# Moving a pair of heads between partitions in sixteen DMAs, with the values three score units behind

## The chip, the cores and the metric

One core of a Trainium2 chip. The metric is the device time of one execution in microseconds (us); less is better. The core has five engines that run at the same time, each through its own list of instructions in order, and wait for one another through semaphores: PE (TensorE, matrix products; PEld is its weight load), DVE (VectorE), ACT (ScalarE), POOL (GpSimd) and SP (SyncE, which here only issues DMAs). Sixteen DMA engines carry the data between the device's memory and the on-chip memory (SBUF), and between places of SBUF. SBUF and PSUM, where PE's results land, have 128 partitions.

## What is computed

One decoder layer for an input x of 8 x 512 x 512 and a context of 8 x 512 x 1024, all float32: a self-attention over the first axis with relative positions, a cross-attention with 8 heads of 64, and a hidden layer of 2048, each followed by an addition and a normalization. The parts that the change touches:

```python
src_trans = einsum('bsf,of->bso', src, W_src) + b_src       # src: the context
tgt_trans = einsum('btf,of->bto', tgt, W_tgt) + b_tgt       # tgt: x after the self-attention
...
scores = einsum('bthd,bshd->bhts', q, k) / sqrt(64)
scores = where(src_mask[:, None, None, :] == 0, -inf, scores)
attn = softmax(scores, axis=-1)
tgt_update = einsum('bhts,bshd->bthd', attn, v).reshape(b, t, 512)
out = einsum('btf,of->bto', concatenate([tgt, tgt_update], axis=2), W_out) + b_out
...
h = relu(einsum('bsd,hd->bsh', x, w1) + b1)                 # then rounded to 8 bits, times w2
```

## The kernel before

There are two phases. The first (to line 617) does the self-attention and projects the context of the sequences 0 to 6 into keys and values; they are kept in the device's memory (`kd`, `vd`), as is the normalized result of the self-attention (`x1d`). The second phase (from line 630) is a loop over the eight sequences t, called steps here. The change is in the second phase.

The second phase is a pipeline over the steps, with an order written out by hand: the scheduler keeps the order in which the program emits instructions on PE, DVE, ACT and SP. In step t, PE does the attention of sequence t, the output projection of t-1 (`project_out`, lines 865 and 869), the query projection of t+1 (`queries`, line 729), the hidden layer of t-1 (`hidden_steps`, line 942) and the second product of the hidden layer of t-2 (`finish`, line 1020). `weave` (line 1091) mixes two lists: `dense` (projections and hidden layer) and the attention steps, which are spread over the dense work by weights; a number with each attention step says how much of the dense list must have been emitted before it.

**Attention.** A sequence has four pairs of heads, c = 0 to 3. A pair is worked on in two units, jj = 0 and 1, each for half of the 512 queries, with the number u = 2 (4t + c) + jj. `scores` (line 740) emits the four products of a unit (line 751) at once and puts the rest on a list of side work: `exponentials` (mask and row minimum on DVE, line 763, exponential on ACT, line 773), `divide` (line 788) and `turn_blocks` (line 800: DVE transposes 32 x 32 blocks within their 32 partitions into `pb`). `run` (line 673) pops side work ahead of each step by a credit of 0.7 of the step's cost, and `settle` (line 659) pops it until a given unit is done.

The blocks of `pb` must then change partitions: `move_blocks` (line 805) issues sixteen DMAs on SP's queue for each unit, one from each quarter g of the 32 partitions to each quarter a, into its half (jj) of `pT`. A pool has two `pb` (one for each unit) and one `pT`. The moves of a unit go on the list `moves`, and `move()` (line 669), which runs ahead of each step, emits them when the pair before has been emitted as attended (`moves[0][0] // 2 <= attended`). `attend` (line 836) makes the sixteen products of the pair (line 845, called av) from pT and the pair's values, and ACT copies the result to `uT`. In `attention_of` (line 1121) the attend of pair c follows the first unit of the pair after it; the last pair of a sequence is attended in the next step.

**Loads on SP's queue.** `load_kv` (line 714) loads a pair's keys and values into two buffers each; `attend_next` (line 1115) emits it for the pair after next, right behind the attend that frees the values' buffer. `load_x1` (line 710) loads `x1d` into one of three buffers; the buffer is free when the results of the sequence three before it have been stored from it (line 1045). The stores of line 1045 are side work of `finish`, and `settle(("y", t - 2))` emits them. `load_w1` (line 917) loads one of eight tiles of the first hidden weight (n = 0 to 7, 896 KB, prepared for a fast product with seven submatrices) into a ring of three (`ring`, part of the tile `ffn`); it is emitted in `p13`, the first products of tile n-2. In step 0 the tiles are loaded raw, POOL makes the sums (line 136 ff) and they are stored in `w1d` (lines 926 to 931); later they come from `w1d` (line 922). SP's list is in order: a DMA that waits for its buffer holds all that are behind it.

**Step 0** has no output projection or hidden layer. Its dense work is the context projection of sequence 7 in eight pieces (`project_context`), between them four conversions of the second hidden weight to 8 bits (`convert`, each of which issues the next load), and the queries of sequence 1. The weights `w_src` for these pieces and the ring `ffn` use the same memory (pool `big`, one buffer), so the ring is taken, and its first two tiles are loaded, at the end of step 0 (lines 1237 to 1257).

Of the kernel before, what the change touches and what calls it, by code (L numbers as in the profile page):

```python
# [42 lines left out]
def decoder_layer(  # L43
# [586 lines left out]
    with ExitStack() as ph:  # L630
# [11 lines left out]
        pbp = pool("pb", 2)  # L642
# [23 lines left out]
        moves = []  # L666
        attended = 0

        def move():
            while moves and moves[0][0] // 2 <= attended:  # L670
                moves.pop(0)[1]()

# [22 lines left out]
        x1, x1T, qT, uT, mb, mvb, kT, v, pT, x2T, hq, mvc = ({} for _ in range(12))  # L695
# [18 lines left out]
        def load_kv(t, c):  # L714
            kT[t, c] = kvd.tile([P, S], F32, tag="kT", name=f"kT{t}_{c}")
            nc.sync.dma_start(kT[t, c], kd[t][:, c, :])
            v[t, c] = kvd.tile([P, ST, P], F32, tag="v", name=f"vx{t}_{c}")
            nc.sync.dma_start(v[t, c], vd[t][:, :, c * P : (c + 1) * P])
# [21 lines left out]
        def scores(t, c, jj):  # L740
            if c == 0 and jj == 0:
                uT[t] = qx.tile([P, EC, S], F32, tag="uT", name=f"uT{t}")
# [4 lines left out]
            for j in js:  # L747
# [10 lines left out]
                pss.append(ps)  # L758

# [32 lines left out]
            def turn_blocks(i):  # L792


                if i == 0:
                    prs.append(
                        pbp.tile([P, 4, ST, 2, 2, 32], F32, tag="pb", name=f"pb{u}")
                    )
                for h in range(2):
                    nc.vector.transpose(  # L800
                        prs[4][:, :, :, h, i, :].rearrange("p a k e -> p k a e"),
# [3 lines left out]
            def move_blocks():  # L805

                if jj == 0:
                    pT[t, c] = ptp.tile(
                        [P, 4, 2, ST, 2, 64], F32, tag="pT", name=f"pT{t}_{c}"
                    )  # L810
                for a in range(4):
                    for g in range(4):
                        nc.sync.dma_start(  # L813
                            pT[t, c][32 * a : 32 * a + 32, g, jj],
                            prs[4][32 * g : 32 * g + 32, a].rearrange(
                                "p k h j e -> p k h (j e)"
# [14 lines left out]
            side.append((u, 1.2, lambda: turn_blocks(0)))  # L831
            side.append((u, 1.2, lambda: divide(1)))
            side.append((u, 1.2, lambda: turn_blocks(1)))
            side.append((u, 0.0, lambda: moves.append((u, move_blocks))))

        def attend(t, c):
# [4 lines left out]
            attended += 1  # L841
            av = mm(f"av{t}_{c}")
# [90 lines left out]
        def hidden_steps(t):  # L933
# [38 lines left out]
            def p13(n):  # L972
                if t * HH2 + n + 2 < T * HH2:
                    load_w1(t * HH2 + n + 2)
# [6 lines left out]
            def p6(n):  # L981
                product(x[n], n, S2, tx[:, 1], False)
# [392 lines left out]
```

## Time and profile before

| | us |
|---|---|
| median of 3 runs (lowest, highest) | 2418.19 (2417.45, 2428.72) |
| the profiled execution | 2425.11 |
| its span | 2423.3 |
| first scores of step 0 (PE, line 751) | 941.7 |
| first second product of the hidden layer in steps 2, 3, 4, 5, 6, 7 (PE, line 1020) | 1279.9, 1451.4, 1618.8 ... 1953.2, 2120.3 |

A table of the stretches of the second phase, from the view that gives the busy time of each engine by stretch (us; PEclk is the clock that PE was granted, as a share of full speed):

| stretch | length | PE busy | DVE busy | ACT busy | PEclk | DMA share |
|---|---|---|---|---|---|---|
| 925 to 1117 (step 0) | 192 | 137.1 | 76.4 | 39.1 | 0.85 | 0.52 |
| 1117 to 1300 (step 1) | 183 | 148.3 | 88.4 | 55.7 | 0.91 | 0.43 |
| 1467 to 1635 (a middle step) | 168 | 148.0 | 90.1 | 57.7 | 0.95 | 0.43 |
| 2135 to 2310 (step 7) | 175 | 133.6 | 79.3 | 48.6 | 0.88 | 0.39 |
| 2310 to 2423 (the end) | 113 | 103.5 | 41.4 | 26.8 | 0.98 | 0.17 |

How to read it: PE is the busiest engine in every stretch. In the middle steps, which repeat, about 20 of 168 us are gaps between its products, and part of its busy time is at a lower clock. The profile says for each gap which event ended it, and the chain that ended last says which work or wait, in order of time, made up the span. A line of the timeline has its start, its duration, the engine, the line of the program, the operation with its output and inputs, how many there were in a row, and in brackets the idle time before it and what ended that.

### The profile page before, as it was taken

What the parts mean: (1) busy time and instruction counts of PE and PEld (TensorE: products, weight loads), DVE (VectorE), ACT (ScalarE), POOL (GpSimd) and SP (SyncE); (2) the same over time, 40 slices, a digit from 0 to 9 for tenths busy, and PEclk for the clock granted to TensorE, in tenths of its full rate; (3) what the DMA queues carried; (4) which work ended last, traced back from release to release, by engine and by line L of the source; (5) the groups of instructions that cost most, each with busy time, mean ns of one, the idle gap of its engine ahead of it and who ended that gap; (6) DMA issues with size and microseconds to landing.
All of it is one profiled execution on the core that took longest, in us unless ns stands there. A gap on an engine that the chain in (4) does not pass through costs nothing.

```text
span 2423.3 us, 22413 instructions
## 1 busy us (share of the span) xinstructions
PE 2130.3 (88%) x7552; PEld 1220.6 (50%) x7552; DVE 1518.1 (63%) x2542; ACT 592.2 (24%) x1325; POOL 167.9 (7%) x156
## 2 busy tenths in 40 slices
PE   8999999999999998866868899898898898996798
PEld 5654664664576665322443463453554544633456
DVE  4799999989999943453436355554564464554324
ACT  2011112001111112221322241332333332413312
POOL 1001100110010000021110001000000000000000
PEclk9999999999999999987989899999999998998899
DMA  8131530342242475533345253453443542633412
GB/s 295 38 109 35 198 141 22 126 145 72 87 161 73 149 254 178 153 97 102 102 142 142 76 167 93 120 143 94 130 129 84 165 133 68 177 75 109 129 35 94
DMA packets 165827, 293.38 MB, mean 121 GB/s; under 512 B 26832, under 2 KB 55504, under 8 KB 165712
## 3 DMA queue, kind: packets, MB, share of 16 engines
q1 hardware_dynamic: 149488, 263.33, 36.1%
q10 hardware_dynamic: 16224, 28.61, 3.2%
q8 instruction: 60, 0.98, 0.2%
q14 instruction: 55, 0.45, 0.1%
HBM read 165.49 MB, written 59.24 MB: 93 GB/s over the span
## 4 chain that ended last, share of the span: by engine, by line
PE 55%; DVE 19%; SPq 11%; DMA 10%; issue 3%; ACT 2%; POOL 0%; DVEq 0%; ACTq 0%; POOLq 0%
SPq L813 10%; PE hx L942 7%; PE av L845 6%; PE px L539 6%; PE pox L865 3%; DVE pv L428 3%; PE hz L942 3%; PE pox L869 3%; PE pz L539 3%; PE o L1020 3%; PE s L751 3%; PE ps_q L338 3%; PE psq L729 3%; PE po L454 2%; DMA pT<-pb 2%
## 5 line engine op out<-in xcount | busy, mean ns | idle before, releaser
L845 PE MATMUL av<-pT,vx 128*64 128x512 f32 x512 | 153.1, 753 | 148.5 <-DMA pT<-pb 148.5
L773 ACT ACTIVATE pe<-pe,nmax 128x512 f32<-128x512 f32 x256 | 183.3, 716 | 237.3 <-DVE nmax L763 227.9
L763 DVE CUSTOM_DVE_ANT_0 pe<-s,mb 128x512 f32<-128x512 f32 x256 | 167.8, 683 | 75.7 <-PE s L751 75.7
L845 PEld LDWEIGHTS av<-pT,vx 128*64 128x64 f32 x512 | 45.9, 172 | 244.4 <-issue 212.5
L800 DVE STREAM_TRANSPOSE pb<-pe 128x512 f32<-128x512 f32 x256 | 166.1, 687 | 1.5 <-issue 1.5
L942 PE MATMUL hx<-ffn 128*128 128x256 f32 x512 | 139.4, 395 | 24.9 <-DVE tm L996 21.7
L428 DVE TENSOR_TENSOR pv<-v,sc 128x2048 f32<-128x2048 f32 x64 | 148.5, 2320 | 2.0
L379 DVE TENSOR_TENSOR pq<-qw,k 128x2048 f32<-128x2048 f32 x64 | 147.3, 2302 | 1.1
L388 DVE TENSOR_REDUCE sc<-pq 128x64 f32<-128x2048 f32 x64 | 146.1, 2282 | 1.4
L942 PE MATMUL hx<-x2T,ffn 128*128 128x256 f32 x512 | 138.3, 393 | 3.7 <-ACT ffn L983 3.7
L751 PE MATMUL s<-kT,qTx 64*128 64x512 f32 x512 | 130.4, 625 | 8.3 <-DVE nmax L763 8.3
L942 PEld LDWEIGHTS hx<-ffn 128*128 128x128 f32 x512 | 91.1, 191 | 73.0 <-DVE tm L996 38.6
L865 PE MATMUL pox<-w_xo,x1Ts 128*128 128x512 f32 x256 | 123.3, 626 | 0.0
L454 PE MATMUL po<-w_o,aoT 128*128 128x512 f32 x256 | 121.7, 620 | 0.7 <-ACT aoT L451 0.7
L979 DVE TENSOR_TENSOR ffn<-hx,ffn 128x256 f32<-128x256 f32 x64 | 27.2, 424 | 150.8 <-PE hx L942 128.7
L788 DVE TENSOR_SCALAR pe<-pe,rden 128x512 f32<-128x512 f32 x256 | 116.3, 497 | 4.5
L729 PE MATMUL psq<-x1Ts,w_tgt 128*128 128x512 f32 x256 | 114.5, 597 | 4.7 <-ACT x1Ts L724 4.7
L338 PE MATMUL ps_q<-w_in,xt 128*128 128x512 f32 x256 | 116.8, 594 | 0.5 <-DVE qw L365 0.5
L869 PE MATMUL pox<-w_xo,uT 128*128 128x512 f32 x256 | 115.1, 592 | 0.0
L338 PE MATMUL ps_k<-w_in,xt 128*128 128x512 f32 x256 | 113.9, 593 | 0.0
L942 PEld LDWEIGHTS hx<-x2T,ffn 128*128 128x128 f32 x512 | 90.5, 190 | 46.5 <-issue 14.0
L338 PE MATMUL ps_v<-w_in,xt 128*128 128x512 f32 x256 | 111.6, 594 | 0.0
(180 smaller groups left out, 3231.7 us busy)
## 6 DMA issues: line engine op xcount, KB each, us to landing
pT<-pb SPq DMA_DIRECT2D x1024, 64.0 KB, 2.0
ffn<-w1d SPq DMA_DIRECT2D x56, 896.0 KB, 4.7
ch<-in_ctxT_dram SPq DMA_DIRECT2D x56, 256.0 KB, 3.3
td<-tx SPq DMA_DIRECT2D x28, 384.0 KB, 3.3
tx<-td SPq DMA_DIRECT2D x28, 384.0 KB, 5.2
r<-in_x_dram SPq DMA_DIRECT2D x32, 256.0 KB, 3.5
xt<-in_xT_dram SPq DMA_DIRECT2D x32, 256.0 KB, 2.6
x1d<-r ACTq DMA_DIRECT2D x32, 256.0 KB, 3.8
```

The source lines that it names most:

```text
L338: nc.tensor.matmul(ps, lhsT=xt[:, e, :], rhs=w_in[:, e, part * E : (part + 1) * E], start=(e == 0), stop=(e == EC - 1),)
L428: nc.vector.tensor_tensor(pr, v_all[:, :, fs].rearrange("p s (h d) -> p s h d", d=D1), sc[:, t, g * HH * T : (g + 1) * HH * T] .rearrange( ...
L454: nc.tensor.matmul(po, lhsT=aoT[:, c * P : (c + 1) * P], rhs=w_o[:, c, :], start=(c == 0), stop=(c == EC - 1),)
L539: nc.tensor.matmul(bank[:, first], lhsT=w7[:, a, f, ps] if part == 0 else b[f][:, ps], rhs=b[f] if part == 0 else w7[:, a, f, :], start=st ...
L729: nc.tensor.matmul(ps, lhsT=w_tgt[:, e, o * P : (o + 1) * P], rhs=x1T[t][:, e, :], start=(e == 0), stop=(e == EC - 1),)
L751: nc.tensor.matmul(ps[:, h, :], lhsT=qT[t][half[h], c, j * P : (j + 1) * P], rhs=kT[t, c][half[h], :], start=True, stop=True,)
L773: nc.scalar.activation(pe, pe, AF.Exp, bias=nmax[:, h : h + 1], scale=-1.0, accum_out=den[:, h : h + 1],)
L813: nc.sync.dma_start(pT[t, c][32 * a : 32 * a + 32, g, jj], prs[4][32 * g : 32 * g + 32, a].rearrange("p k h j e -> p k h (j e)"),)
L845: nc.tensor.matmul(av[half[h], :], lhsT=v[t, c][:, s, half[h]], rhs=pT[t, c][:, :, :, s, h].rearrange("p g i q -> p (g i) q"), start=(s == 0),
L865: nc.tensor.matmul(po, lhsT=x1T[t][:, e, js], rhs=w_xo[:, e, :], start=(e == 0), stop=False)
L869: nc.tensor.matmul(po, lhsT=uT[t][:, e, js], rhs=w_xo[:, EC + e, :], start=False, stop=(e == EC - 1),)
L942: nc.tensor.matmul(ps[:, 0:W], lhsT=ring[:, (t * HH2 + n) % RING, a, e, :], rhs=b[:, e, :], start=start and e == 0, stop=e == 1, skip_grou ...
```

## The change

- `pb` holds a whole pair (both units) and has one buffer in place of two; the sixteen moves are issued once for a pair. Each moves 32 partitions x 4 KB where each moved 32 x 2 KB, and the order of the quarters is rotated (g = (a + i) % 4).
- A pair's attend follows the second unit of the pair after it, so its values are three units behind its scores; the weights in `attention_of` are set anew, and the second unit of a step may be emitted ahead of the last attend of the step before. `divide` and `turn_blocks` change places.
- Keys and values are loaded apart, each put on a list `later` and issued two calls of `move()` later: the keys after the pair's second score unit, the values after its attend. `load_w1` goes from `p13` to `p6`, the step behind it.
- `x1` of the sequence t+1 is loaded inside step t from step 1 on (before: from step 2 on), and one transpose of it (`turns[1]`) goes behind the last output projection.
- Two of the eight context pieces of sequence 7 go from step 0 to step 1, and the ring is taken (`take_ring`), with its first two tiles, behind them.
- The buffer of `uT` is taken in `attend` and not in `scores`; a list `pb` of the bias is renamed `pbo`.

```diff
-        pbp = pool("pb", 2)
+        pbp = pool("pb", 1)
...
-        moves = []
+        moves, later = [], []
         attended = 0
 
         def move():
-            while moves and moves[0][0] // 2 <= attended:
+            while moves and moves[0][0] <= attended:
                 moves.pop(0)[1]()
+            for item in later:
+                item[0] -= 1
+            while later and later[0][0] < 0:
+                later.pop(0)[1]()
...
+            p = u // 2 + 2
+            if jj == 1 and p < T * EC:
+                later.append([2, lambda: load_k(p // EC, p % EC)])
...
             def turn_blocks(i):
-                if i == 0:
-                    prs.append(
-                        pbp.tile([P, 4, ST, 2, 2, 32], F32, tag="pb", name=f"pb{u}")
+                if i == 0 and jj == 0:
+                    pb[t, c] = pbp.tile(
+                        [P, 4, 2, ST, 2, 2, 32], F32, tag="pb", name=f"pb{t}_{c}"
                     )
...
             def move_blocks():
-                if jj == 0:
-                    pT[t, c] = ptp.tile(
-                        [P, 4, 2, ST, 2, 64], F32, tag="pT", name=f"pT{t}_{c}"
-                    )
-                for a in range(4):
-                    for g in range(4):
+                pT[t, c] = ptp.tile(
+                    [P, 4, 2, ST, 2, 64], F32, tag="pT", name=f"pT{t}_{c}"
+                )
+                for i in range(4):
+                    for a in range(4):
+                        g = (a + i) % 4
                         nc.sync.dma_start(
-                            pT[t, c][32 * a : 32 * a + 32, g, jj],
-                            prs[4][32 * g : 32 * g + 32, a].rearrange(
-                                "p k h j e -> p k h (j e)"
+                            pT[t, c][32 * a : 32 * a + 32, g],
+                            pb[t, c][32 * g : 32 * g + 32, a].rearrange(
+                                "p i k h j e -> p i k h (j e)"
                             ),
                         )
...
             side.append((("e", u), 1.0, lambda: exponentials(1, 1)))
-            side.append((u, 1.2, lambda: turn_blocks(0)))
             side.append((u, 1.2, lambda: divide(1)))
-            side.append((u, 1.2, lambda: turn_blocks(1)))
-            side.append((u, 0.0, lambda: moves.append((u, move_blocks))))
+            side.append((u, 1.3, lambda: turn_blocks(0)))
+            side.append((u, 1.3, lambda: turn_blocks(1)))
+            if jj == 1:
+                side.append((u, 0.0, lambda: moves.append((u // 2, move_blocks))))
...
             def p13(n):
-                if t * HH2 + n + 2 < T * HH2:
-                    load_w1(t * HH2 + n + 2)
...
             def p6(n):
+                if t * HH2 + n + 2 < T * HH2:
+                    load_w1(t * HH2 + n + 2)
...
             if p < T * EC:
-                load_kv(p // EC, p % EC)
+                later.append([2, lambda: load_v(p // EC, p % EC)])
...
-                    need = queried if u == 2 * EC else begun + (t > 0)
-                    weight = 0.5 if u % 2 == 0 else 1.0
-                    if u == 2 * EC - 1 and t in (0, T - 1):
-                        weight = 3.0
-                    steps += [(2.0, need, lambda n=n: scores(*n), weight)]
-                if u % 2 == 0 and u < 2 * EC:
-                    c = u // 2 - 1
-                    steps += [(3.8, projected, lambda c=c: attend_next(t, c), 0.5)]
+                    need = queried if u == 2 * EC else begun + (u > 1 and t > 0)
+                    steps += [[2.0, need, lambda n=n: scores(*n), 1.0]]
+                if u % 2 == 1 and u > 1:
+                    steps[-1][3] -= 0.7
+                    f = lambda c=u // 2 - 1: attend_next(t, c)
+                    weight = 2.2 if u == 2 * EC - 1 and t + 1 == T else 0.7
+                    steps += [(3.8, projected, f, weight)]
...
-                    early = 0 if t == 1 else NJ if t + 1 < T else NJ // 2
-                    if early:
-                        dense += sum(done[: early - 1], [])
+                    early = NJ if t + 1 < T else NJ // 2
+                    first = sum(done[: early - 1], [])
+                    second = done[early - 1]
+                    if t == 1:
+                        first = of(6.9, pieces[-2])
+                        second = of(6.9, pieces[-1]) + of(0.0, take_ring)
+                    dense += first
                     begun = len(dense)
-                    dense += values_of(t - 1)
-                    if early:
-                        dense += done[early - 1]
-                    dense += out4[0]
+                    dense += values_of(t - 1) + second + out4[0]
                     dense += of(0.0, settle, ("y", t - 2)) + out4[1]
-                    if 1 < t < T - 1:
+                    if t + 1 < T:
                         dense += of(0.0, load_x1, t + 1)
-                    dense += out4[2] + turns[0] + turns[1] + out4[3]
+                    dense += out4[2] + turns[0] + out4[3] + turns[1]
```

## The prediction

> **What bounds the kernel now.** I read the busy times and the chain that ended last, then who waits for whom on PE, then PE and SP side by side over one pass of the loop over t (a step).
>
> ```profile
> PE 2130.3 (88%) x7552; PEld 1220.6 (50%) x7552; DVE 1518.1 (63%) x2542; ACT 592.2 (24%) x1325; POOL 167.9 (7%) x156
> PE 55%; DVE 19%; SPq 11%; DMA 10%; issue 3%; ACT 2%; POOL 0%; DVEq 0%; ACTq 0%; POOLq 0%
> ```
> PE is the bound, yet SP's queue and DMA make up 21% of the chain. The PE waits say where:
>
> ```profile
> PE av L845 <- DMA pT<-pb: 148.5, 21, 30.7
> PE xtr L723 <- DMA x<-x1d: 28.6, 5, 6.1
> PE hx L942 <- DVE tm L996: 21.7, 42, 0.5
> ```
> Total, times, longest. 177 us are waits for two transfers: the turned probabilities pT, and the next x1. The third row (0.5 us each) is inside the hidden layer and not touched. PE's timeline in step 4:
>
> ```profile
> 1499.24 1.97 PE L723 MATMUL xtr<-ident,x 128*128 128x128 f32 x8 [5.68 <-DMA x<-x1d]
> 1501.00 5.11 PE L865 MATMUL pox<-w_xo,x1Ts 128*128 128x512 f32 x8
> 1549.76 6.36 PE L845 MATMUL av<-pT,vx 128*64 128x512 f32 x16 [7.18 <-DMA pT<-pb]
> 1587.80 3.65 PE L845 MATMUL av<-pT,vx 128*64 128x512 f32 x16 [2.00 <-DMA pT<-pb]
> ```
> The gap is in brackets. After 7.18 us of idling the same av takes 6.36 instead of 3.65 us; after 5.68 us, pox takes 5.11 instead of its usual 3.60 and xtr 1.97 instead of 1.3. After 2.00 us nothing is lost. So a wait over some 3 us costs another 2.2 to 2.7 us. SP's timeline of the same step:
>
> ```profile
> 1483.10 10.27 SPq L813 DMA_DIRECT2D pT<-pb  x16
> 1493.41 0.58 SPq L712 DMA_DIRECT2D x<-x1d  x1
> 1557.70 10.49 SPq L813 DMA_DIRECT2D pT<-pb  x16
> 1568.29 4.42 SPq L922 DMA_DIRECT2D ffn<-w1d  x2
> ```
> Sixteen moves (one of a pair's two units) hold the queue for 10.3 us: 0.64 us each. x1 is issued behind such a burst, at 1493.41, and PE, ready for it at 1493.56, waits until it lands.
>
> **The moves: 512 of 128 KB for 1024 of 64 KB.** At 0.64 us each, a pair costs SP 10.3 us instead of 20.6, 32 x 10.3 = 330 us of queue less, none of it PE time by itself. That holds if twice the bytes do not slow them:
>
> ```profile
> pT<-pb SPq DMA_DIRECT2D x1024, 64.0 KB, 2.0
> ffn<-w1d SPq DMA_DIRECT2D x56, 896.0 KB, 4.7
> x<-x1d SPq DMA_DIRECT2D x8, 1024.0 KB, 5.9
> ```
> ```profile
> 1516.00:1523.00 7.00, 7.00 (x19) 2.96 (x19) 2.92 (x6) 0.75 (x2) 0.29 (x1) 1.00 0.46 106
> ```
> The last two figures are DMA share and GB/s inside a burst: 0.46 and 106. From 64 KB in 2.0 us to 1024 KB in 5.9 is 4.1 us per MB, so 64 KB more are 0.3 us; and 128 KB per 0.64 us are 205 GB/s, what a stretch with ffn in it moved (201 at a share of 0.72). No row shows 4 KB pieces. Lower bound of a pair's burst: 9.4 us (16 issues at their 0.59 us median). Upper: 20 us, if 106 GB/s were all that these copies reach. I take 10.3 us plus 2.3 to land, since a share of 0.46 leaves room for twice the bytes.
>
> **Three units behind.** By the compiled order both score units of the next pair now stand ahead of each av, before only the first. A burst starts when the pair's last transpose is done and av of the pair before has ended, whichever is later, and lands 12.6 us on. Counting PE's own durations (o 3.45, s 1.92, av 3.59, pox 6.87, psq 3.45, a hidden product 0.87 us) from the step's first o, call it 0: av of pair 0 comes at 52 with its burst over at 38; av of pair 1 at about 90, its burst over at 73; pairs 2 and 3 have 14 us or more in hand. So in steps 2 to 6 the av waits go: 9.2 us plus 2.7 of slow clock.
>
> **What is behind the bursts now.** x1: the last transpose of pair 0 ends at 25.5 (scores at 12.3, three evictions, o's 2.4 us on DVE, division, 4 x 0.65); burst to 36; vx 0.6; four stores to 38.4. The x1 buffer is the one these stores read, so its load waits for their landing, 2.4 us: issue at 40.5, landing 46.3 (5.8 later, as in the rows above). PE wants it at 43.8: 2.5 us of idling, no clock loss, for 5.7 + 2.2 before. Bounds 0 to 6.
> The w1 load: it is issued a step later (p6), which puts the load for n=4 behind pair 2's burst. That burst begins 5.2 us after av of pair 1 (one product, ACT's copy and DVE's c12, transposes, tm, transposes stand in DVE's order): 15.5 us after av the load is issued, at 20.2 it lands (4.7). PE comes to hy of n=4 after 15 products, one s and two 0.5 us waits: 16.1. A new wait of 4.2 us, with 2.2 of slow clock 6.4. Before, the same load at 1568.29 was in time for hy at 1575.73, and PE had lost its time at av instead. Bounds 0 (the burst begins with av's end) to 12.
> A middle step is 167.4 us (1467.22 to 1634.62); less 9.2 + 5.7 + 2.7 + 2.2 it is 147.6; plus 2.5 + 6.4 it is 156.5. Four such steps gain 10.9 each, step 2 (171.6 us) gains 15.1: **58.7 us**.
>
> **pb with one buffer.** DVE's transposes of the next pair wait for the whole burst to land, and everything behind them on DVE waits too. In the steps above they come 3 to 5 us after landing, or hold only adds that PE doesn't need for 2 us. Cost 0; without that margin it is the excess, at the c11 add of the hidden layer.
>
> **Steps 0 and 1.** The longest wait is the end of step 0:
>
> ```profile
> 1109.47 6.34 PE L845 MATMUL av<-pT,vx 128*64 128x512 f32 x16 [30.72 <-DMA pT<-pb]
> ```
> ```profile
> 1092.61 0.91 SPq L712 DMA_DIRECT2D x<-x1d  x1
> 1093.62 14.20 SPq L813 DMA_DIRECT2D pT<-pb  x16
> ```
> SP spent 1075.11 to 1092.13 on two w1 tiles (loads, POOL's sums, stores), and the pair's last burst stood behind. They move behind the last context piece in step 1. From s at 941.66 to step 2's first o at 1279.85 are 338.2 us; waits for pT (46.2 + 23.8), w1 (5.8) and some 18 of slow clock are 94, leaving 244. New: step 0 becomes a chain per pair (burst 12.6, then four transposes, four exponentials, divisions, four transposes, some 12 us on DVE: 25 us for some 24 us of PE work), and the last conversions of w2 wait for a load behind a burst: I take 20 us of waits in all (10 to 40). Step 1: the two w1 tiles hold SP 17 us after the last context piece, so burst and x1 come later; x1 lands some 10 us after PE wants it, with clock 12. n=4's load goes through POOL here (8.4 instead of 4.7 us): 8 + 2. 244 + 20 + 12 + 10 = 286: **52 us**, and I take **48** for what is counted roughly here.
>
> **Step 7.** From 2120.3 to 2310.3 it takes 190.0 us; four waits for pT (4.0, 12.7, 13.3, 3.55) and 11 of slow clock go. Here n=4's load stands ahead of the burst and n=5's lands 3 us early; the last av (at 130 us) comes as its burst lands. 190 - 33.6 - 11 = 145.4, with 2 for that close call 147: **43 us**. The end (113 us) has no pT.
>
> **Sum.** 58.7 + 48 + 43 = 150 us. The profiled execution took 2425.1 us (span 2423.3): 2275. It lies 6.9 us over the median 2418.2, so 2268 is forecast.
>
> **Rivals.**
> (a) The new waits do not come: av of pair 1 finds its burst earlier, n=4 in time, x1 too. Without the 8.9 us in five steps, 22 in step 1 and 15 of step 0's 20: 2268 - 82 = 2186. For it: each is short by 2 to 8 us only. Against: the queue's order is fixed.
> (b) Bursts are somewhat slower, 14 us, with w1, x1 and stores sharing the engines. One us of burst costs 2 per middle step (x1 and n=4), 3 in step 1, 4 in step 0: 17 in all; 3.7 x 17 = 63: 2331. For it: 205 GB/s on top of the other traffic.
> (c) Slower: the burst is bound by its bytes at the 106 GB/s seen, 20 us a pair. Place: SP's queue, ahead of x1 and n=4. 9.7 x 17 = 165: 2433, above before. It decides from 10.3 + 150/17 = 19 us a burst. Against: the share of 0.46 and the landing times.
> This is also what a rule would do. The Trainium skill, "Perfetto Trace Analysis", DMA Optimizations, says that with idle DMA engines splitting DMAs into smaller chunks may let the whole finish sooner; merging two units is the reverse. By that rule the time is that of (c); the trace bears it out only in that the first unit's move can no longer run under the second unit.
> (d) One pb buffer binds: DVE holds the c11 adds in front of PE. If landing is 5 us later than counted, two pairs in each of seven steps lose 5 us: 2268 + 70 = 2338. For it: DVE's order puts the transposes ahead of c11. Against: margins of 3 to 5 us. The Trainium skill, same page, Optimization Strategy, says that a gap that repeats can mean too few buffers for the next tile; by that rule it is (d).
> (e) The moves do not get earlier and the waits change places: 2418. The compiled order speaks against it.
>
> **Chances.** Forecast 0.60, (a) 0.10, (b) 0.14, (c) 0.07, (d) 0.06, (e) 0.03. The range goes from just above (a) to just above (b) and (d): 2200 to 2345, which leaves out (c), (e) and the outer part of (a). 0.5% (12 us, about the spread of the three runs) is what tells a change from none: faster 0.89, same 0.03, slower 0.08.
>
> **What would show it.** Right: 512 moves at about 0.64 us; av waits for pT under 30 us in all; x1 waits of 2 to 3 us in steps 2 to 6; a wait of hy for ffn of about 4 us once a step; steps of some 156 us. Wrong: bursts over 14 us; DVE idle ahead of L800's transposes with hx waiting for ffn (c11); steps above 165 us.

## The result and the profile after

The changed kernel takes 2308.65 us (median of 4 runs, 2306.65 to 2311.81), the kernel before 2417.82 us beside it (4 runs): a ratio of 0.954 with a 95% interval of 0.951 to 0.957, 109 us less. The forecast was 2268 with a range of 2200 to 2345. The profiled execution of the changed kernel took 2308.47 us, span 2306.7, and lies at its median.

The page of the changed kernel: busy times, the shares of the chain that ended last, and the moves with their size and the time from issue to landing:

```profile
PE 2115.4 (92%) x7552; PEld 1216.8 (53%) x7552; DVE 1522.1 (66%) x2542; ACT 591.6 (26%) x1325; POOL 166.1 (7%) x156
PE 62%; DVE 20%; DMA 10%; ACT 3%; SPq 3%; issue 2%; POOL 0%; DVEq 0%; ACTq 0%
...
pT<-pb SPq DMA_DIRECT2D x512, 128.0 KB, 2.4
```

PE does the same work at nearly the same busy time (2130.3 before); its share of the chain went from 55% to 62%, and SP's queue from 11% to 3%. Who waits for whom on PE in the changed kernel (total, times, longest, in us):

```profile
PE hx L954 <- DVE tm L1008: 26.3, 48, 0.7
PE xtr L731 <- DMA x<-x1d: 25.6, 6, 10.2
PE hy L954 <- DMA ffn<-w1d: 14.6, 6, 3.8
...
PE x2tr L731 <- ACT x2T L732: 10.9, 8, 1.6
PE hz L954 <- ACT tm L975: 8.9, 7, 3.7
...
PE av L857 <- DMA pT<-pb: 7.6, 2, 4.1
...
PE hx L954 <- DVE qTx L744: 4.7, 6, 0.8
```

The 148.5 us for pT are 7.6 now. The wait for x1 is still there, that for the w1 load (hy) is new (0.3 us before), and three rows of waits for ACT and DVE at the start of the hidden layer are new or have grown (before: x2tr 2.0 us, hz 3.7, qTx none). SP's timeline of step 3:

```profile
1431.43 10.06 SPq L822 DMA_DIRECT2D pT<-pb  x16
...
1442.22 2.13 SPq L1057 DMA_DIRECT2D out_dram<-x  x4
1447.46 0.38 SPq L718 DMA_DIRECT2D x<-x1d  x1
...
1511.43 10.10 SPq L822 DMA_DIRECT2D pT<-pb  x16
1521.63 10.22 SPq L934 DMA_DIRECT2D ffn<-w1d  x3
```

Sixteen moves of 128 KB hold the queue for 10.1 us, 0.63 us each, much as sixteen of 64 KB did. Where other transfers are under way a burst takes up to 13.9 us; the mean of the 32 is 10.6. Behind pair 0's burst stand the stores and x1, behind pair 2's the load for n=4. PE in the same step, x1 landing late, then the waits at the start of the hidden layer, then n=4:

```profile
1452.96 0.66 PE L731 MATMUL xtr<-ident,x 128*128 128x128 f32 x4 [2.73 <-DMA x<-x1d]
...
1483.30 1.14 PE L731 MATMUL x2tr<-ident,x 128*128 128x128 f32 x8 [1.57 <-ACT x2T L732]
...
1490.39 1.13 PE L954 MATMUL hx<-x2T,ffn 128*128 128x256 f32 x4 [0.78 <-DVE qTx L744]
1492.37 1.13 PE L954 MATMUL hz<-x2T,ffn 128*128 128x256 f32 x4 [0.85 <-ACT tm L975]
1494.48 1.13 PE L954 MATMUL hx<-ffn 128*128 128x256 f32 x4 [0.97 <-DVE ffn L989]
...
1526.40 2.07 PE L954 MATMUL hy<-x2T,ffn 128*128 128x256 f32 x4 [2.54 <-DMA ffn<-w1d]
```

After the last wait four products take 2.07 instead of 1.03 us. Where the time came from, by stretch, in the two profiled executions (us; idle is the length less PE's busy time):

| stretch | before | after | gain | forecast | PE idle before, after |
|---|---|---|---|---|---|
| ahead of step 0's scores | 941.7 | 940.0 | 1.7 | 0 | |
| steps 0 and 1 | 338.2 | 299.2 | 39.0 | 48 | 87.0, 45.4 |
| steps 2 to 6 | 840.5 | 811.2 | 29.3 | 58.7 | 101.9, 78.5 |
| step 7 | 190.0 | 144.0 | 46.0 | 43 | 45.4, 9.5 |
| the end | 113.0 | 112.4 | 0.6 | 0 | |

Most of the gain is idle time of PE (101 us in the three middle rows; PE's busy time went down by 14.9 us in all, with a mean granted clock of 0.973 instead of 0.948), and most of what is missing against the forecast is missing in the steps 2 to 6: step 2 took 166.8 us, and there were 160.7, 162.9, 157.7 and 163.0 us for steps 3 to 6 (mean 161.1) against 156.5 for each.

### The profile page after: what moved, and what is told of

It reads as the page before. It is cut to its first block, busy times and chain, and to the rows that moved or that the text cites. A ratio compares the mean times of both kernels' runs of the same rounds, so it can differ in the third digit from the quotient of the medians.

```text
span 2306.7 us, 21733 instructions
## 1 busy us (share of the span) xinstructions
PE 2115.4 (92%) x7552; PEld 1216.8 (53%) x7552; DVE 1522.1 (66%) x2542; ACT 591.6 (26%) x1325; POOL 166.1 (7%) x156
## 4 chain that ended last, share of the span: by engine, by line
PE 62%; DVE 20%; DMA 10%; ACT 3%; SPq 3%; issue 2%; POOL 0%; DVEq 0%; ACTq 0%
PE hx L954 9%; PE px L539 7%; PE av L857 5%; PE pox L877 4%; PE hz L954 4%; PE pox L881 4%; PE s L757 4%; PE pz L539 4%; PE psq L737 3%; DVE pv L428 3%; PE o L1032 3%; SPq L822 3%; PE ps_q L338 3%; PE po L454 2%; DMA ch<-in_ctxT_dram 2%; PE hy L954 2%
## 5 line engine op out<-in xcount | busy, mean ns | idle before, releaser
L809 DVE STREAM_TRANSPOSE pb<-pe 128x512 f32<-128x512 f32 x256 | 161.9, 681 | 32.5 <-DMA pT<-pb 25.7
L954 PE MATMUL hx<-x2T,ffn 128*128 128x256 f32 x512 | 142.4, 402 | 8.4 <-DVE qTx L744 4.7
L428 DVE TENSOR_TENSOR pv<-v,sc 128x2048 f32<-128x2048 f32 x64 | 148.5, 2321 | 2.0
L954 PEld LDWEIGHTS hx<-ffn 128*128 128x128 f32 x512 | 91.5, 194 | 85.2 <-DVE tm L1008 46.8
L857 PE MATMUL av<-pT,vx 128*64 128x512 f32 x512 | 121.2, 617 | 8.5 <-DMA pT<-pb 7.6
L1032 PE MATMUL o<-w2q,hq 128*128 128x512 fp8e4 x480 | 108.1, 383 | 2.6 <-DVE o L1042 2.6
L999 DVE TENSOR_TENSOR ffn<-hz,ffn 128x256 f32<-128x256 f32 x64 | 27.2, 425 | 100.3 <-ACT ffn L995 100.3
```

The costliest lines, as they stand in the source:

```text
L428: nc.vector.tensor_tensor(pr, v_all[:, :, fs].rearrange("p s (h d) -> p s h d", d=D1), sc[:, t, g * HH * T : (g + 1) * HH * T] .rearrange( ...
L857: nc.tensor.matmul(av[half[h], :], lhsT=v[t, c][:, s, half[h]], rhs=pT[t, c][:, :, :, s, h].rearrange("p g i q -> p (g i) q"), start=(s == 0),
L954: nc.tensor.matmul(ps[:, 0:W], lhsT=ring[:, (t * HH2 + n) % RING, a, e, :], rhs=b[:, e, :], start=start and e == 0, stop=e == 1, skip_grou ...
L1032: nc.tensor.matmul(po, lhsT=hq[t][:, c, j * P : (j + 1) * P], rhs=w2q[:, c, :], start=(c == 0), stop=(c == HC - 1),)
```

## The experiments

All are edits of the changed kernel, whose time is called 2308.65 here. Each was timed against the kernel before on its own chip (2417.67 to 2418.67 us). In the profiled executions the first scores of step 0 start between 933.1 and 943.7 us (940.0 in the changed kernel), though no edit touches what stands ahead of them. So of a gain of 10 us or less these profiles can't say that it comes from the edit.

### Moves of 64 KB with the three-unit lag

```diff
-                        nc.sync.dma_start(pT[t, c][32 * a : 32 * a + 32, g], ...)
+                        for i2 in range(2):
+                            nc.sync.dma_start(pT[t, c][32 * a : 32 * a + 32, g, i2], ...)
```

> The changed kernel, but a pair is moved in 32 DMAs of 64 KB (2 KB pieces) instead of 16 of 128 KB; the three-unit lag and everything else stays. Theory 1 (the queue time of a burst sets when x1, the stores and the w1 load for n=4 land, and in the early steps when av may run): a burst becomes some 20.6 us, 10.3 more, and every wait behind it grows by as much: by my reckoning 17 us per us of burst, 2308 + 175 = 2483 us, above the kernel before; x1 waits near 13 us and hy waits for ffn near 13 us a step. Theory 2 (the lag alone brings the gain, and merging only tidies the queue): waits for pT stay gone, the other loads have slack, 2300 to 2350 us.

2509.17 us, ratio 1.038 (1.036 to 1.040). Theory 1, and rather more than it said. SP's timeline and PE's waits:

```profile
1556.10 20.14 SPq L823 DMA_DIRECT2D pT<-pb  x32
...
1597.39 23.44 SPq L823 DMA_DIRECT2D pT<-pb  x32
```
```profile
PE xtr L731 <- DMA x<-x1d: 82.1, 6, 20.1
PE hy L955 <- DMA ffn<-w1d: 71.8, 6, 13.4
PE av L858 <- DMA pT<-pb: 45.8, 6, 12.1
```

The same bytes in twice as many DMAs double the burst (10.1 to 20.1 us; the second row holds 3.3 us more, in which the burst's second DMA waits for the pair's last transposes) and put x1 and the w1 load some 12 us late in each step. 200.5 us for some 10 us of burst are 20 us per us of burst; I had reckoned 17. So with moves of the old size and number the lag makes the kernel slower than before, here with one `pb` buffer and with a pair's moves issued together.

### Two units behind, with moves of 128 KB

```diff
-                    need = queried if u == 2 * EC else begun + (u > 1 and t > 0)
+                    need = queried if u == 2 * EC else begun + (t > 0)
...
-                if u % 2 == 1 and u > 1:
+                if u % 2 == 0 and u < 2 * EC:
```

> The changed kernel with 16 moves of 128 KB a pair, but the values again two units behind the scores, with the order of scores and av of the kernel before. Theory 1 (the lag hides the landing: a burst of 10.3 us starts only when the second unit's transposes are done, some 12 us after its scores, and lands 2.3 later): av waits for pT three times a step, 3 to 10 us each with slow clock behind it, some 12 to 20 us a step: 2400 to 2460 us. Theory 2 (a shorter burst is enough): av waits for pT under 40 us in all, within 20 us of 2308.

2465.18 us, ratio 1.019 (1.017 to 1.021): Theory 1, a little above its range. av waits for pT for 167.9 us in all. PE in step 4 of this run:

```profile
1558.31 5.75 PE L857 MATMUL av<-pT,vx 128*64 128x512 f32 x16 [8.36 <-DMA pT<-pb]
...
1598.20 6.27 PE L857 MATMUL av<-pT,vx 128*64 128x512 f32 x16 [4.00 <-DMA pT<-pb]
```

The first burst was issued from 1546.39 to 1556.43 and av was ready before it. Before the change half of a pair's moves ran under its second unit; merged, all wait for that unit. So in this kernel neither half pays without the other: with the rest of the change in place, merging without the lag is 47.5 us slower than the kernel before, the lag without merging 91.5 us slower, the two together 109 us faster. Whether the lag alone would pay with two `pb` buffers and a unit's moves issued as soon as it is done, as before, no run shows.

### The w1 load on the POOL queue

```diff
-                nc.sync.dma_start(w, w1d[n])
+                nc.gpsimd.dma_start(w, w1d[n])
```

> The changed kernel with the load of a summed w1 tile issued from the POOL queue instead of SP's, all else as it is. Theory 1 (n=4's load stands behind pair 2's burst, and PE's clock falls after even a 2.5 to 4 us wait): hy waits for ffn<-w1d (14.6 us in all, 6 of them) go to under 3 us, and the slow products behind them (some 2 us each) go as well: 2308 - 12 - 10 = some 2286 us. Rival A (the wait goes, but the slow clock has another cause and stays): 2296 us, granted clock in steps 3 and 4 still 0.96 to 0.98. Rival B (the load is late because the DMA engines are shared with the burst, not because of the queue): hy waits stay, 2308 us.

2359.89 us, ratio 0.976 (0.973 to 0.979): 51 us slower than the changed kernel, outside all three expectations. The load is no longer late, but now it runs beside pair 2's burst. SP, DVE and PE in step 3:

```profile
1513.93 14.67 SPq L822 DMA_DIRECT2D pT<-pb  x16
...
1535.82 1.30 DVE L809 STREAM_TRANSPOSE pb<-pe 128x512 f32<-128x512 f32 x2 [6.01 <-DMA pT<-pb]
1537.05 0.39 DVE L989 TENSOR_TENSOR ffn<-hx,ffn 128x256 f32<-128x256 f32 x1
...
1537.49 2.07 PE L954 MATMUL hx<-ffn 128*128 128x256 f32 x4 [5.15 <-DVE ffn L989]
```

POOL issues two of the loads beside this burst, at 1514.30 and 1523.23. The burst takes 14.7 instead of 10.1 us and lands some 7 us after its last issue instead of 2.4. DVE's next transposes need the single `pb` buffer, wait 6.0 us for that landing, and the c11 add behind them holds PE for 5.2 us. In all, DVE waited 76.7 us for pT's landing (25.7 in the changed kernel). How late landings stretch the issuing shows in SP's own waits, where the changed kernel has no such row:

```profile
SPq L822 <- DMA pT<-pb: 62.1, 36, 6.1
```

By the traces of the changed kernel and of this run, no DMA on SP's queue is issued before the one eight places ahead of it has landed. A landing after 2.4 us is over by then; here moves land after 8 to 9 us, and the queue stops. Why they land late shows in the stretches view. The last two columns are the DMA engines' busy share and GB/s, first inside a burst of the changed kernel, then inside this one:

```profile
1433.00:1440.00 7.00, 7.00 (x22) 2.90 (x19) 5.19 (x15) 3.36 (x7) 0.00 (x0) 1.00 0.94 207
```
```profile
1522.00:1528.60 6.60, 6.10 (x28) 4.85 (x26) 3.78 (x12) 4.13 (x11) 0.70 (x1) 1.00 1.01 247
```

With 64 KB the share in a burst was 0.46; with 128 KB it is 0.94, so there is little room for a load beside a burst. SP's order, which lets the load start only after the burst, had protected it. The Trainium skill, "Trainium Kernel Development and Optimization", Key Constraints, says in general that DMAs from the queues of SP, ACT and POOL run on the same sixteen engines and interleave, and that issuing from several saves only issue time. The runs agree: POOL's queue saved the wait for SP and cost 51 us.

### The stores and x1 on the POOL queue

```diff
-            nc.sync.dma_start(x1[t], x1d[t].rearrange("j p e -> p j e"))
+            nc.gpsimd.dma_start(x1[t], x1d[t].rearrange("j p e -> p j e"))
...
-                    nc.sync.dma_start(out[n0 : n0 + P, :], y)
+                    nc.gpsimd.dma_start(out[n0 : n0 + P, :], y)
```

> The changed kernel with the four stores of the output and the load of x1 (which waits for their landing) issued from the POOL queue instead of SP's. Theory 1 (x1 is late only because the stores stand behind pair 0's burst): normalised rows are ready some 6 us before the burst ends, so x1 lands some 5 us earlier; xtr waits for x1 (25.6 us in all, 10.2 of it in step 1) fall under 4 us, and the slow clock behind them goes: 2308 - 22 - 8 = 2278 us. Rival (the loads and stores now run beside the burst on the same engines and land late, or delay the burst): xtr waits stay above 15 us or av waits for pT grow by as much, 2300 to 2315 us.

2293.04 us, ratio 0.948 (0.947 to 0.950), 15.6 us less: in part Theory 1. The xtr waits for x1 fell from 25.6 to 1.3 us in all. The burst of pair 0, which now runs beside the stores and x1, suffers: in steps 2 to 6 it takes 11.9 to 12.4 us and lands 5.2 to 8.1 us after its last issue (10.0 to 11.3 and 2.3 us before the edit). av's waits for pT don't grow by it (7.4 us in all, 7.6 before the edit). But only 2.4 us of a middle step went (161.1 to 158.7), less than the 3.2 us wait that did: the slow clock stayed (PE was busy for 146.7 us of a step, 145.8 before the edit). And in step 1 another wait stands in the place of x1's 10.2 us, here in the order DVE, PE:

```profile
1121.56 2.49 DVE L809 STREAM_TRANSPOSE pb<-pe 128x512 f32<-128x512 f32 x4 [20.27 <-DMA kT<-kd]
```
```profile
1127.53 5.59 PE L857 MATMUL av<-pT,vx 128*64 128x512 f32 x16 [12.27 <-ACT x1Ts L732]
```

The first burst of step 1 stands behind the two w1 tiles and is issued from 1107.64 to 1118.6; DVE's next transposes wait for its landing because there is one `pb` buffer (the releaser named is only the last semaphore that the profile saw). The row minima behind them on DVE come late, so do ACT's exponentials, behind these ACT's copies of the x1 transposes, and behind the copy av, which takes its PSUM bank from the same pool. In the changed kernel DVE waits there too (13.4 us), covered by the wait for x1.

### The w1 load one step earlier

```diff
             def p13(n):
+                if t * HH2 + n + 2 < T * HH2:
+                    load_w1(t * HH2 + n + 2)
...
             def p6(n):
-                if t * HH2 + n + 2 < T * HH2:
-                    load_w1(t * HH2 + n + 2)
```

> The changed kernel with the w1 load issued in p13 again, as before the change, still from SP's queue. By the compiled order the load for n=4 then stands ahead of pair 2's burst. Theory 1 (my prediction: the load is late because it is behind the burst): hy waits for ffn<-w1d go from 14.6 us to under 3, and the slow clock that follows them, 3 to 4 us in four of five steps, goes too: steps of some 155 us, 2280 us. Rival (the burst now runs at a DMA share of 0.94 by itself, so that 0.9 MB beside it stretches it to some 14 us, pT lands late and the single pb buffer holds DVE in front of the c11 adds, as the run with w1 on the POOL queue showed): hx waits for ffn (c11) of 20 us or more, 2310 to 2345 us.

2282.5 us, ratio 0.944 (0.942 to 0.946), 26 us less: Theory 1. The hy waits for w1d are gone and steps 3 to 6 take 157.2 us on average. SP in step 3:

```profile
1504.00 0.32 SPq L934 DMA_DIRECT2D ffn<-w1d  x1
1504.42 11.44 SPq L822 DMA_DIRECT2D pT<-pb  x16
```

A 0.9 MB load right ahead of the burst lengthens it by 1.3 us, since the eighth move waits for its landing, and the burst lands 4.0 us after its last issue instead of 2.3. The single `pb` buffer still bears that: DVE waits 32.2 us in all for pT's landing (25.7 in the changed kernel). So the part of the change that issues this load a step later costs 26 us.

### The third pair's scores 3.5 us earlier

```diff
                     weight = 2.2 if u == 2 * EC - 1 and t + 1 == T else 0.7
+                    if u == 3 and 0 < t < T - 1:
+                        weight = 0.5
```

> The changed kernel with a smaller weight (0.5 instead of 0.7) for av of pair 0 in steps 1 to 6, which puts the scores of the third pair's first unit one projection (3.5 us) earlier, ahead of psq of o=2 instead of directly ahead of the x2 transposes. Theory 1 (the new small waits at the start of the hidden layer, 4.1 us a step, come from this unit's exponentials standing ahead of the x2T copies on ACT and of the x2 sums on DVE): waits of x2tr for ACT (10.9 us), of hx for qTx (4.7) and of hz for tm (8.9) fall to under 8 together, some 3 us a step in six steps: 2290 us. Rival (the order of these few instructions costs as much wherever they stand): 2303 to 2313 us.

2274.39 us, ratio 0.941 (0.939 to 0.943), 34 us less, twice what was expected, but for the expected reason only in part. Of the 34 us 6 stand ahead of step 0's scores in the profiled execution, where the edit does nothing. PE's waits for ACT's x2T copies fell from 10.9 to 2.9 us in all, and hz's for tm from 8.9 to 3.7, but qTx's rose from 4.7 to 16.6. The three together are 23.2 us instead of 24.5, where under 8 were expected:

```profile
1468.86 1.15 PE L731 MATMUL x2tr<-ident,x 128*128 128x128 f32 x8 [0.24 <-ACT x2T L732]
...
1477.76 1.25 PE L954 MATMUL hx<-x2T,ffn 128*128 128x256 f32 x4 [2.59 <-DVE qTx L744]
```

With two other rows that shrank (hx's waits for the adds of `ffn` and tm) the small waits of a middle step are 2 us less. The larger part, 2.9 us a step, came from a wait I hadn't thought of here: the earlier unit brings pair 2's burst forward, from 105.4 us into step 3 (1511.43 less 1406.01) to 101.4, and the hy waits for w1d go with it, from 14.6 to 0.5 us.

### The early steps undone, and put otherwise

```diff
-                    for piece in pieces[:-2]:
+                    for piece in pieces:
...
-                    if t == 0:
+                    if t < 2:
                         load_x1(t + 1)
...
-                        first = of(6.9, pieces[-2])
-                        second = of(6.9, pieces[-1]) + of(0.0, take_ring)
+                        first = second = []
...
                 weave(dense, attention_of(t, begun, projected, queried))
+                if t == 0:
+                    take_ring()
```

> The changed kernel with the two early steps as they were: all eight pieces of the last context product in step 0, the hidden layer's ring and its first two w1 tiles at the end of step 0, and the load of x1 for step 2 at the start of step 1. Theory 1 (my prediction: the two w1 tiles hold SP some 17 us ahead of the last pair's burst, which av of that pair then waits for): the x1 wait of 10.2 us in step 1 goes, and av at the start of step 1 waits some 25 us with slow clock behind it: start of step 2's first o (1239.2) 10 to 25 us later, 2320 to 2335 us. Rival (what steps 0 and 1 gained is the lag and the merged moves alone): within 5 us of 2308, or below it by the x1 wait.

2300.3 us, ratio 0.952 (0.949 to 0.954): the rival. Both of Theory 1's waits are as it said, yet step 2's first o comes at 1231.6, 7.6 us earlier than in the changed kernel (4.4 us, counted from step 0's first scores). The intervals of the two kernels overlap. PE, then SP:

```profile
1080.60 6.64 PE L857 MATMUL av<-pT,vx 128*64 128x512 f32 x16 [22.05 <-DMA kT<-kd]
```
```profile
1061.21 0.91 SPq L718 DMA_DIRECT2D x<-x1d  x1
1062.22 15.08 SPq L822 DMA_DIRECT2D pT<-pb  x16
```

What the changed kernel saves at av it pays at x1 (10.2 us) and, as I read it, in a step 0 with less work under its pairs. The burst takes 15.1 us here, beside x1's load and the store of a w1 tile, all from one queue. The next run keeps all pieces in step 0 and x1's load at the start of step 1, but takes the ring behind av:

```diff
-                        first = of(6.9, pieces[-2])
-                        second = of(6.9, pieces[-1]) + of(0.0, take_ring)
+                        first, second = [], of(0.0, take_ring)
```

> The changed kernel with all eight pieces of the last context product in step 0 and the load of x1 for step 2 at the start of step 1, as before the change, but the ring's first two w1 tiles in step 1, behind av of step 0's last pair. Theory 1 (the change's early steps lose where the two w1 tiles stand ahead of x1 and of a burst; with all of step 0's pieces under the chain of pairs and the tiles behind av, neither av nor xtr waits): av's 22.0 us of the run with the early steps undone go without the 10.2 us for x1 coming back, step 2's first o at some 1210 instead of 1239.2, 2280 us. Rival (the tiles now hold the first burst of step 1 for 17 us, and av of that pair or x1 waits as long): 2295 to 2310 us.

2288.14 us, ratio 0.946 (0.944 to 0.948): Theory 1. The two waits are gone (the longest for pT is 6.3 us), step 2's first o is at 1213.7, 25.5 us earlier than in the changed kernel (21.8 counted from step 0's first scores). 4 us of it are lost in steps 2 to 6, where PE was busy for 737.2 instead of 732.6 us at a granted clock of 0.97 instead of 0.98.

### Loads of keys and values at once

```diff
-                later.append([2, lambda: load_k(p // EC, p % EC)])
+                later.append([0, lambda: load_k(p // EC, p % EC)])
```

and the same for `load_v`.

> The changed kernel with the loads of k and v issued one call of the queue's counter after the step that frees their buffer (0 instead of 2 steps later). Theory 1 (what follows such a load on SP's queue waits for PE anyway: the burst waits for the same av, and lands with time in hand): 2303 to 2316 us. Rival (a k or v load that waits for PE holds SP in front of a burst, x1 or w1 load, each of which is short by nothing): hy and xtr waits grow by 2 us or more a step, 2320 us or more.

2298.37 us, ratio 0.951 (0.949 to 0.954). That is below the range of either theory. The interval overlaps the changed kernel's, so this part of the change is worth nothing that these runs can tell, or costs a few us; the rival is excluded.

### The edits together

Three: the w1 load in p13, stores and x1 on POOL, the earlier scores.

> Three edits on the changed kernel together: the w1 load issued in p13, the stores and x1's load issued from the POOL queue, and the third pair's first scores one projection earlier. If each wait is separate, the gains add: 2293 (x1 and stores on POOL, measured) less some 28 (hy waits and slow clock) less some 18 (small waits): 2247 us, steps of some 150 us. Rival (the w1 load stretches the burst and DVE is held, so that the waits change places): 2285 us or more.

2250.84 us, ratio 0.931 (0.929 to 0.933): 58 us less, as expected. By themselves the three gave 15.6, 26 and 34 us, 76 together: the second and the third both remove hy's wait, which can be gained only once. With the early steps of the run above as well:

> The three edits run together before (2251 us), with the early steps of z1 as well. If the early steps are separate from the rest: av's 12.4 us in step 1 and the slow clock behind it go, some 25 us: 2226 us. If not, 2245 us or more.

2228.68 us, ratio 0.922 (0.920 to 0.924): 189 us below the kernel before, the best version measured. Its steps 4 and 6 in the stretches view (the first two figures are length and PE busy, the third from the end the granted clock), and the same steps of the changed kernel:

```profile
1527.12:1677.18 150.06, 142.41 (x546) 77.58 (x545) 89.74 (x215) 57.23 (x130) 10.73 (x11) 1.00 0.49 135
...
1827.08:1976.51 149.43, 142.16 (x546) 77.63 (x544) 89.97 (x215) 57.40 (x130) 11.70 (x11) 1.00 0.48 134
```
```profile
1566.70:1729.63 162.93, 146.08 (x545) 79.28 (x544) 90.03 (x215) 57.21 (x130) 8.81 (x6) 0.98 0.45 124
...
1887.35:2050.35 163.00, 147.76 (x546) 80.24 (x545) 90.08 (x215) 57.20 (x130) 8.47 (x6) 0.97 0.45 124
```

Without the waits for x1 and w1 PE has its full clock in these steps and is busy for 142.2 to 142.4 us; of the 7.6 us of idling left in a step, 2.6 is qTx's. The last run tried to take that away (weight 0.3 and, for the third pair's first unit, 1.5):

> As the run with four edits together, but the third pair's first scores another projection earlier (weight 0.3) and its second unit three products later (weight 1.5). Theory (the 2.6 us for which hx waits for qTx in each step come from divisions and transposes of this unit standing ahead of qTx's eviction on DVE): that wait falls under 1 us in steps 2 to 6, some 2 to 3 us a step less: 2212 us. Rival (the same DVE work then stands ahead of something else that PE wants): 2226 us or more.

2245.18 us, ratio 0.929 (0.927 to 0.931), 16.5 us more: the rival. The qTx wait stayed (2.7 us in each of five steps): two steps of the unit's divisions, the second of which waits for ACT, now stand ahead of the eviction, where one and a transpose had stood. And the waits for the x2T copies came back in part (9.5 us in all).

## Why the prediction was right, and where it fell short

**The burst.** Right: 512 moves at 0.63 us, 10.1 us a pair, landing 2.4 us later. It also holds that twice the bytes had room, but only just: the DMA engines are busy for 0.94 of a burst.

**Three units behind.** Right: av's waits for pT went from 148.5 to 7.6 us; the run with two units shows that it is the lag that does it.

**What stands behind the bursts.** Right in kind and nearly in size: x1 2.7 to 3.8 us in steps 2 to 6 (forecast 2.5), n=4's load 2.5 to 3.8 (4.2). The run with the load in p13 and the one with x1 on another queue confirm the places.

**The sum of a middle step failed.** 147.6 + 2.5 + 6.4 = 156.5 became 161.1: 147.6 + 3.2 (x1) + 2.9 (hy) + 4.2 + 3.1. The 4.2 are the small waits at the start of the hidden layer, to which the sum gave nothing (0.8 of them were there before; 0.7 of a new wait for tm, not in the 4.2, about make up for that). I moved the scores three units against av but took ACT's and DVE's order around them as it had been; the third pair's exponentials now stand directly ahead of the x2T copies and the x2 sums. ACT in step 3:

```profile
1480.67 1.28 ACT L782 ACT_TABLE_LOAD   x1 [10.89 <-DVE nmax L772]
1481.97 0.72 ACT L782 ACTIVATE pe<-pe,nmax 128x512 f32<-128x512 f32 x1
...
1482.69 1.05 ACT L732 COPY x2T<-x2tr 128x512 f32<-128x512 f32 x2
```

The first exponential brings a load of ACT's function table with it, of 1.28 us. The kernel before has the same load in each step (34 in all in both), but there it and its exponentials were done before the copies were wanted; here it stands between PE's transposes and their copies, and it is most of the 1.6 us for which x2tr waits. The run with the earlier scores bears the place out: with the unit 3.5 us earlier x2tr's wait is 0.24 us again and hz's is gone. It doesn't take all of the 4.2 away, since the unit's divisions then delay qTx's eviction (2.6 us a step). The 3.1 are slow clock (mean PE busy 145.8 in steps 3 to 6, less 142.7 in the best run), of which 2.2 were forecast, at hy alone. "No clock loss" for x1's wait was the wrong part. The rule behind it, a loss over some 3 us and none after 2.00, left out a row of the trace of before, in its step 2:

```profile
1292.56 5.25 PE L845 MATMUL av<-pT,vx 128*64 128x512 f32 x16 [2.19 <-DMA pT<-pb]
```

After 2.19 us the same av took 5.25 instead of 3.65 us, while after one of 2.30 us, at 1017.18, it took 3.65. In the changed kernel PE waits for x1 and for hy's tile ten times in steps 2 to 6, for 2.5 to 3.8 us; four of these waits, with the 7 us that follow each (the third figure from the end is the clock):

```profile
1364.13:1371.13 7.00, 6.48 (x18) 4.79 (x19) 2.59 (x6) 2.35 (x6) 0.00 (x0) 0.60 0.36 118
...
1526.40:1533.40 7.00, 6.48 (x22) 5.15 (x23) 2.73 (x7) 2.95 (x7) 0.00 (x0) 0.79 0.34 112
...
1776.72:1783.72 7.00, 7.00 (x20) 3.41 (x21) 2.71 (x8) 2.82 (x7) 1.27 (x1) 1.00 0.00 0
1848.51:1855.51 7.00, 6.48 (x29) 5.35 (x30) 4.19 (x9) 2.95 (x7) 0.00 (x0) 1.00 0.55 197
```

Those waits were 2.79, 2.54, 2.87 and 2.58 us: length alone does not decide. Eight of the ten are followed by a clock of 0.60 to 0.79, which at 0.76 costs 1.7 us of the 7.

**Step 2** was forecast to gain 15.1 us and gained 4.6. Beside the terms above, o waits 2.57 us there for a DVE add that is held behind transposes waiting for pT's landing: the one place behind step 0 where the single `pb` buffer, costed at 0, shows on PE in the changed kernel (in step 1 the wait for x1 covers it).

**Steps 0 and 1.** 39 us instead of 48, for a reason partly wrong. That the two w1 tiles cost av its wait is shown (22 us when put back). That moving them was a gain is not: undone, the kernel was no slower. With these steps as before the change, the stretch from step 0's first scores to step 2's first o still takes 294.8 us instead of 338.2, so the gain doesn't come from them; I take it to be that of the lag and the merged moves. The sum also took 2.2 us twice: of the 23.8 us of waits for pT in step 1, the 2.19 us above stand in step 2.

**Step 7**: 46.0 us (43). **The base**: 6.9 us were taken off because the profiled execution of before lay over its median; that of the changed kernel doesn't. These 7 us and 33 of the sum are the 41 us between forecast and result. The result lies in the range because the range is wide: the steps 2 to 6 gained half of what the sum said.

**The rivals.** (c): the run with 64 KB moves has its 20 us bursts, for another cause, the number of issues, and its outcome: slower than before, as its tipping point of 19 us said. The rule of the Trainium skill named there ("Perfetto Trace Analysis", DMA Optimizations), that splitting DMAs may let the whole finish sooner when the DMA engines are generally idle, gives the wrong sign here: with the engines half idle (0.46), merging pairs of DMAs halved the queue's time and splitting them again doubled it, since SP's 0.63 us per issue bound. (d): not in the changed kernel, save in step 2 (and hidden in step 1); as soon as something stretches the burst, it is what decides (the w1 load on POOL). (a), (b) and (e) did not come.

**Left open.** Why a wait of 2.6 us costs clock one time and not another. Whether two `pb` buffers would make the w1 load on POOL pay: two of them were not tried; nor were these loads on ACT's queue, so how much of the late landing is POOL's queue and how much the sharing of engines isn't separated, though loads and stores on SP's own queue stretched a burst to 15.1 us as well.

## What to carry to other kernels

Where small DMAs are bound by their issue, as these of 64 KB were, bigger ones can cost the queue no more as long as the DMA engines have room; look at the busy share inside a burst, and keep other loads out of it once it is near 1. Merging transfers delays the first of them, so here it needed the lag, and the lag needed the merging: judge such parts together, and then try each of the rest alone, since here one part that came along (the w1 load a step later) cost 26 us, and another (the early steps) gained nothing and could be put some 20 us better. A single row of a trace doesn't make a rule: look for rows that speak against it before a term of the sum rests on it. When work is moved in a hand-written order, go through the in-order lists of the engines that serve it too, at the place where it lands, table loads included.

## What the runs showed of the hardware that was not expected

- A PE wait of 2.5 to 3.8 us is followed by a granted clock of 0.60 to 0.79 in eight of ten cases in the changed kernel, and in two of five 2.6 us waits of the best run. In the kernel before it was 0.77 after 2.19 us, but 1.00 after 2.30. The Trainium skill, "TensorE: Matmul & The Clock Gate", What's actually happening, puts the drop to half clock after an idle window of about 3.4 us that runs freely. That the length alone does not decide fits this; that waits of 2.19 and 2.54 us, shorter than the window, are enough in some cases isn't explained by it.
- A DMA of 32 partitions from SBUF to SBUF held SP for 0.63 us with 64 KB and with 128 KB alike, and landed after 2.0 and 2.4 us.
